# A four-layer graph kernel: order of the first loads, W1·a as one block, later weight sums, six last graphs turned on TensorE, and bv added to x3 early

## Chip, core and metric

The kernel runs on one core of one Trainium2 chip. The metric is the time of one execution on the device in microseconds, the median of several runs. "Before" took 2840.91 us (three runs, 2839.7 to 2845.04). Everything is float32.

## What is computed

128 graphs of 128 nodes with 512 features pass through four layers. Each layer adds its result to its input and normalizes over the features:

```python
# layer 0: out[n] = max over nodes of relu(adj @ x), with a shift b
x = layernorm(x + L0(x, adj, b))
# layer 1: graph attention; h = x @ W, s1 = h @ a1, s2 = h @ a2
e   = leaky_relu(s1[:, None] + s2[None, :], 0.2) * adj
x = layernorm(x + elu(softmax(e) @ h + beta * h))
# layer 2: graph convolution
x = layernorm(x + (adj @ x) @ weight + bias)
# layer 3: attention with 8 heads of 64, masked where adj == 0
q, k, v = x @ Wq + bq, x @ Wk + bk, x @ Wv + bv
x = layernorm(x + softmax(q @ k.T / 8 + mask) @ v)
```

## The kernel before

One graph fills the 128 partitions (nodes), with 512 features along the row. There is no loop over layers in the code. A small planner (`Plan`, L23 to L124) holds a list of TensorE steps (`l0`, `zT`, `z`, `yT`, `y`, `xT`, q/k/v, `sc`, `pT`, `avT`, `av`; L935 to L957), a place for each in the order, an assumed cost, and the marks and buffers that it needs. Each step is a generator. It issues its matmuls and then asks for engine time with `yield dve(...)`, `act(...)`, `pool(...)` or `sp(issue, landing)`. The planner advances an imagined clock and so fixes, while the program is built, in which order each engine's instructions stand. On the chip every engine runs its own list in order and waits for data alone; the planner's microseconds are no waits there. A buffer given back with `plan.give` is free in the plan, and the real dependency is kept by semaphores.

**Start.** The five weight matrices (1 MB each) are loaded by ScalarE's queue right away, in one DMA each (`load_w`, L214). The rows `a_bc`, `bias2_bc` and `bv_bc` (each broadcast to 128 partitions, 256 KB) and the small columns are loaded by POOL's queue. SP loads adj and the graphs, two x buffers deep (`load_x`, L208). `w1_a` (L274 to L301) computes W1·a1 and W1·a2, so that layer 1's s1 and s2 come straight from x: for each half and each of four blocks of W1, a multiply with a row sum on VectorE (L285), a diagonal matrix of that column (L288) and a product with ones (L289), and at the end a copy to `wa_bc` (L295). `weight_sums` (L307) prepares q, k and v for a seven-product form of the 2x2 block product: four POOL adds for each matrix (L324), Wq scaled first on ScalarE (L316).

**Layers 0 to 2.** `l0` (L373) multiplies with adj, takes the maximum (L381), adds it (L387), normalizes, and forms s2 and s1 (L400). `attention` (L435) makes the softmax (L439 to L455). `l1_zT` and `l1_out` give z = (att x) W1 (L482, L496, L506 to L512). `l2_yT` and `l2_out` do layer 2 (L536, L496, L578). `layernorm` (L330) is a VectorE statistic (L333, L335), three small POOL steps (L338, L340, L342) and one ScalarE pass (L344). Its result x3 is stored to HBM in the layout of the turn and kept there for the residual.

**Layer 3.** Four graphs form a group. `seven` computes q, k and v of a group in seven steps each (L660), from x transposed (`xTh`) and POOL differences of it (`T`, L566). `l3_scores` (L758) writes the scores of a graph to a score bank in PSUM, of which there is one (`"sc": 1`), adds the mask on VectorE into `pr` (L780), takes the row maxima (L786) and runs eight exp on ScalarE (L790). For all but the last `LATE` = 4 graphs the weights are transposed by a *turn* (`turn`, L346): a DMA to HBM (L354), a DMA back (L358), and a 32x32 block transpose on VectorE (L365). There is one `pr` buffer of this kind. `l3_avT` (L835) then forms the output transposed (L843), copies it (L855) and turns it back the same way. `fetch` (L610) brings x3 back from HBM as `x3r` (L614). POOL scales by the softmax sums (L868), adds x3r (L869) and adds bv (L871); then come the last normalization and the store (L877).

For the last four graphs `pr` lies in a buffer of `xTh`, TensorE transposes it (`l3_pT`, L822), ScalarE and VectorE copy it out of PSUM (L829, L831), and `l3_av` (L880) computes the output untransposed (L890) with the sums as a 65th column, divides (L902, L903), and adds x3r and bv on POOL (L913, L916).

Of the kernel before, what the change touches and what calls it, by code (L numbers as in the profile page):

```python
# [9 lines left out]
F32 = mybir.dt.float32  # L10
# [4 lines left out]
P = 128  # L15
# [112 lines left out]
def kernel(  # L128
# [25 lines left out]
    NQ = P // Q  # L154
    EARLY, LATE = GB, GB

# [16 lines left out]
    small = ctx.enter_context(tc.tile_pool(name="small", bufs=5))  # L173
    plan = Plan({**sb_bufs, **ps_bufs, **hbm_bufs, "va": NV})

# [24 lines left out]
    def sp(us, landing):  # L200
        return ("SP", us, landing)
# [6 lines left out]
    def load_x(b):  # L208
        x0[b] = yield from get("x0", [P, C], f"x0_{b}")
        yield sp(0.35, 2.5 if b > 2 else 7.0)  # L210
        nc.sync.dma_start(out=x0[b], in_=x[b])
        plan.mark(("x0", b))

    def load_w(w, name):  # L214
        t = const.tile([P, NCC, C], F32, tag=name, name=name)
        nc.scalar.dma_start(out=t, in_=w.rearrange("(c p) f -> p c f", p=P))
        return t

    def load_row(v, name):
        t = const.tile([P, C], F32, tag=name, name=name)  # L220
        nc.gpsimd.dma_start(out=t, in_=v.partition_broadcast(P))
        return t

# [5 lines left out]
    a_flat = a1.rearrange("f o -> (f o)")  # L229
    a_bc = []  # L230
    for i in range(2):
        t = sb_tile("xp", [P, C], f"a_bc{i}")
        nc.gpsimd.dma_start(out=t, in_=a_flat[i * C : (i + 1) * C].partition_broadcast(P))
        a_bc.append(t)
        plan.left["xp"] -= 1
    b0_col = load_col(b0, 1, "b0_col")
    w1_sb = load_w(w1, "w1_sb")
# [4 lines left out]
    w2_sb = load_w(w2, "w2_sb")  # L242
    wq_sb = load_w(wq, "wq_sb")
    wk_sb = load_w(wk, "wk_sb")
    wv_sb = load_w(wv, "wv_sb")
    bias2_bc = load_row(bias2, "bias2_bc")
    bv_bc = load_row(bv, "bv_bc")
    bq_col = load_col(bq, NCC, "bq_col")
    bk_col = load_col(bk, NCC, "bk_col")


# [19 lines left out]
    wa_bc = [const.tile([P, C], F32, tag=f"wa_bc{i}", name=f"wa_bc{i}") for i in range(2)]  # L271
    plan.engine["DVE"] = 7.0

    def w1_a():  # L274

        yield sp(0.0, 9.0)
        for i in (1, 0):
            yield "mm"
            ps = ps_tile("mm", f"ps_wa{i}")
            for c in range(NCC):  # L280
                junk = yield from get("junk", [P, C], f"wa_junk{i}_{c}")
                dg = yield from get("att", [P, P], f"wa_diag{i}_{c}")
                yield dve(1.1)
                col = small.tile([P, 1], F32, tag="col", name=f"wa_col{i}_{c}")
                nc.vector.scalar_tensor_tensor(  # L285
                    junk, w1_sb[:, c, :], 1.0, a_bc[i], ALU.mult, ALU.mult, accum_out=col
                )
                nc.vector.tensor_scalar(dg, ident, col, None, ALU.mult)  # L288
                nc.tensor.matmul(ps[:, c * P : (c + 1) * P], ones, dg, start=True, stop=True)  # L289
                plan.give("junk")  # L290
                plan.give("att")
            plan.give("xp")
            yield ("PE", 0.5, 0.0)
            yield dve(0.7)
            nc.vector.tensor_copy(wa_bc[i], ps)  # L295
# [275 lines left out]
    def l2_out(b):  # L571
        s = st[b]
        yT = s.pop("yT")
        ps = product(f"y_{b}", lambda c: yT[:, c * P : (c + 1) * P], lambda c: w2_sb[:, c, :])
        plan.give("yT")
        xp = yield from get("xp", [P, C], f"xp2_{b}")
        yield dve(0.7)
# [32 lines left out]
    def fetch(b, tag):  # L610
# [147 lines left out]
    def l3_scores(b):  # L758
# [54 lines left out]
    def l3_pT(i):  # L813
# [9 lines left out]
        plan.give("xTh")  # L823
        s["pT"] = sb_tile("pT", [P, H, P], f"pT_{b}")
# [10 lines left out]
    def l3_avT(b):  # L835
# [44 lines left out]
    def l3_av(i):  # L880
# [12 lines left out]
        if hh == 0:  # L893
            s["o"] = sb_tile("oT", [P, H, HD], f"o_{b}")
        else:
# [19 lines left out]
        plan.give("oT")  # L915
        nc.gpsimd.tensor_tensor(xp, xp, bv_bc, ALU.add)  # L916
        yield from last(b, xp)
# [12 lines left out]
    def av_waits(b):  # L930
# [23 lines left out]
            lambda i: av_waits(late_av(i)),  # L954
            lambda i: {"mm": 1, "oT": 1 - i % 2}, l3_av,
        ),
# [3 lines left out]
    for b in range(sb_bufs["x0"]):  # L960
        plan.at(1.0, load_x(b))
    plan.at(0.0, w1_a())
    for n, w in (("q", wq_sb), ("k", wk_sb), ("v", wv_sb)):
        plan.at(0.0, weight_sums(n, w))
# [32 lines left out]
```

## Time and profile before

| what | value |
|---|---|
| median of three runs | 2840.91 us |
| profiled execution | 2842.72 us, its span 2840.7 us |
| granted TensorE clock, mean | 0.985 |
| TensorE busy | 2736.5 us, 96% of the span |
| VectorE busy | 2268.5 us, 80% |
| ScalarE busy | 1577.9 us, 56% |
| POOL busy | 1397.2 us, 49% |
| DMA | 395.42 MB, mean 139 GB/s |

The span runs from the first to the last instruction of the core. In the profile's names PE is TensorE, DVE is VectorE, ACT is ScalarE, POOL is GpSimd and SP the engine that issues most DMAs; a "q" behind a name is an engine's queue. A row of the timeline gives the start, the length, the engine, the line, the operation with output and input, and in brackets the idle time ahead of it and what ended that.

### The profile page before, as it was taken

The page shows a single profiled execution, that of the slowest core. Times are in us where ns is not written, and L with a number is a line of the kernel's source. Part 1 is how long each engine was busy: PE and PEld are TensorE (multiplying, and loading weights), DVE is VectorE, ACT ScalarE, POOL GpSimd, SP SyncE. Part 2 cuts the span into 40 slices and gives each one's busy share as a digit, 9 for nine tenths or more (in the row PEclk, how much of TensorE's full clock was granted, in tenths as well). Part 3 has the DMA queues.
Part 4 walks back from the last instruction along what each step waited for, and adds up shares of the span by engine and source line. Part 5 has one row for each costly group of instructions (what it writes and reads, how often), then busy time and mean ns, then how long its engine had stood idle before and what let it go on. Part 6 is the DMA issues. An engine that isn't in the chain of part 4 may idle for free.

```text
span 2840.7 us, 43148 instructions
## 1 busy us (share of the span) xinstructions
PE 2736.5 (96%) x13901; PEld 1939.3 (68%) x13901; DVE 2268.5 (80%) x4290; ACT 1577.9 (56%) x4205; POOL 1397.2 (49%) x2198
## 2 busy tenths in 40 slices
PE   4999999999999999999999999999999999999985
PEld 2667767667667677777666767767677767777674
DVE  6678787788888888788888878778888788778755
ACT  2555555555555655555555556555555555555543
POOL 4435455455455555445554545545445555445534
PEclk8999999999999999999999999999999999999996
DMA  3224444454444454454454544544454544444443
GB/s 114 59 71 132 141 152 141 129 159 142 140 149 149 135 166 140 136 155 134 147 150 143 160 146 132 163 143 137 136 162 139 166 133 147 150 136 143 135 133 122
DMA packets 462178, 395.42 MB, mean 139 GB/s; under 512 B 88832, under 2 KB 378752, under 8 KB 461952
## 3 DMA queue, kind: packets, MB, share of 16 engines
q1 hardware_dynamic: 458864, 386.37, 44.6%
q10 hardware_dynamic: 2640, 5.24, 0.5%
q8 instruction: 110, 1.80, 0.3%
q0 software_dynamic: 448, 1.05, 0.1%
q14 instruction: 116, 0.95, 0.1%
HBM read 219.75 MB, written 172.82 MB: 138 GB/s over the span
## 4 chain that ended last, share of the span: by engine, by line
PE 83%; DVE 11%; DMA 2%; POOL 1%; issue 1%; ACT 1%; SPq 0%; POOLq 0%; DVEq 0%; ACTq 0%
PE ps_z L496 14%; PE ps_y L496 13%; PE ps_k_chain L660 7%; PE ps_q_chain L660 7%; PE ps_v_chain L660 7%; PE ps_av L843 4%; PE ps_zT L482 4%; PE ps_sc L764 4%; PE ps_k_pair L660 4%; PE ps_yT L536 4%; PE ps_v_pair L660 3%; PE ps_q_pair L660 3%; PE psA L378 3%; DVE pT L365 2%; PE ps_q_first L660 2%; PE ps_v_first L660 2%
## 5 line engine op out<-in xcount | busy, mean ns | idle before, releaser
L338 POOL TENSOR_SCALAR ve<-mv 128x1 f32<-128x1 f32 x512 | 129.9, 254 | 819.8 <-DVE mv L335 739.4
L790 ACT ACTIVATE pr<-pr,nm 128x128 f32<-128x128 f32 x1024 | 397.8, 392 | 126.1 <-DVE nm L786 124.6
L496 PE MATMUL ps_y<-w_sb,yT 128*128 128x512 f32 x1024 | 463.6, 595 | 3.9 <-ACT yT L542 3.3
L496 PE MATMUL ps_z<-w_sb,zT 128*128 128x512 f32 x1024 | 463.3, 595 | 1.0 <-ACT zT L488 1.0
L344 ACT ACTIVATE x<-xp,nmr,rstd 128x512 f32<-128x512 f32 x384 | 310.5, 809 | 159.9 <-POOL nmr L342 158.6
L333 DVE BATCH_NORM_STATS2 stats<-xp 128x6 f32<-128x512 f32 x512 | 345.1, 674 | 37.7 <-ACT xp L387 22.6
L496 PEld LDWEIGHTS ps_z<-w_sb,zT 128*128 128x128 f32 x1024 | 193.2, 191 | 203.2 <-issue 196.6
L496 PEld LDWEIGHTS ps_y<-w_sb,yT 128*128 128x128 f32 x1024 | 190.4, 190 | 204.8 <-issue 195.6
L340 POOL TENSOR_TENSOR rstd<-ve,nhalf 128x1 f32<-128x1 f32 x512 | 302.2, 590 | 42.6
L868 POOL TENSOR_TENSOR xp<-xp,rd 128x512 f32<-128x512 f32 x124 | 131.5, 1061 | 368.5 <-DVE xp L365 207.1
L365 DVE STREAM_TRANSPOSE pT<-turn_pr 128x1024 f32<-128x1024 f32 x124 | 254.1, 2049 | 2.3 <-DMA turn_pr<-turn_hbm_pr 2.3
L400 DVE SCALAR_TENSOR_TENSOR junk<-x,wa_bc 128x512 f32<-128x512 f32 x256 | 196.0, 766 | 53.2 <-ACT x L344 51.7
L506 ACT ACTIVATE elu_r<-ps_z 128x512 f32<-128x512 f32 x128 | 76.1, 594 | 248.2 <-PE ps_z L496 247.9
L522 POOL TENSOR_TENSOR x2b<-x,bias_bc 128x512 f32<-128x512 f32 x128 | 165.4, 1292 | 83.9 <-ACT x L344 83.8
L790 ACT ACTIVATION_READ_ACCUMULATOR pr<-pr,nm 128x1 f32 x992 | 187.7, 189 | 0.0
L764 PEld LDWEIGHTS ps_sc<-kTh,qTh 64*128 64x128 f32 x2048 | 128.3, 192 | 66.6 <-issue 37.4
L342 POOL TENSOR_SCALAR nmr<-mv,rstd 128x1 f32<-128x1 f32 x512 | 146.6, 286 | 53.0
L764 PE MATMUL ps_sc<-kTh,qTh 64*128 64x128 f32 x2048 | 153.2, 290 | 17.0 <-DVE pr L780 16.9
L510 DVE SCALAR_TENSOR_TENSOR xp<-ps_z,x 128x512 f32<-128x512 f32 x128 | 88.1, 688 | 100.3 <-ACT elu_r L506 100.2
L871 POOL TENSOR_TENSOR xp<-xp,bv_bc 128x512 f32<-128x512 f32 x124 | 163.0, 1314 | 9.7
L780 DVE TENSOR_TENSOR pr<-ps_sc,mask 128x1024 f32<-128x1024 f32 x128 | 154.8, 1209 | 15.0 <-DMA turn_hbm_pr<-pr 7.3
L869 POOL TENSOR_TENSOR xp<-xp,x3r 128x512 f32<-128x512 f32 x124 | 161.6, 1304 | 9.7
(147 smaller groups left out, 5863.8 us busy)
## 6 DMA issues: line engine op xcount, KB each, us to landing
turn_hbm_pr<-pr SPq DMA_DIRECT2D x124, 512.0 KB
turn_pr<-turn_hbm_pr SPq DMA_DIRECT2D x124, 512.0 KB
x<-in_x_dram SPq DMA_DIRECT2D x128, 256.0 KB
out_dram<-xp SPq DMA_DIRECT2D x128, 256.0 KB
turn_hbm_x<-x SPq DMA_DIRECT2D x124, 256.0 KB
turn_x<-turn_hbm_x SPq DMA_DIRECT2D x124, 256.0 KB
turn_hbm_o<-oT SPq DMA_DIRECT2D x124, 256.0 KB
turn_o<-turn_hbm_o SPq DMA_DIRECT2D x124, 256.0 KB
```

What stands on the lines that cost most here:

```text
L333: nc.vector.bn_stats(stats, src)
L340: nc.gpsimd.tensor_tensor(rstd, ve, nhalf, ALU.pow)
L344: nc.scalar.activation(dst, src, AF.Identity, bias=nmr, scale=rstd)
L365: nc.vector.transpose(dst.rearrange("p n (c a) -> p a n c", a=NQ), t)
L400: nc.vector.scalar_tensor_tensor(junk, x1, 1.0, wa_bc[i], ALU.mult, ALU.mult, accum_out=col)
L496: nc.tensor.matmul(ps, lhsT(c), rhs(c), start=(c == 0), stop=(c == NCC - 1))
L522: nc.gpsimd.tensor_tensor(xb, x2, bias2_bc, ALU.add)
L660: nc.tensor.matmul(ps[:, m, :], lhsT, rhs, start=fresh and m + k == 0, stop=m + k == 2, skip_group_check=not fresh)
L764: nc.tensor.matmul(ps[:, h % 2, f, :], heads["q", g][j // 2][r : r + HD, f, j % 2 * P : (j % 2 + 1) * P], heads["k", g][j // 2][r : r + HD ...
L790: nc.scalar.activation(pr_h[:, i], pr_h[:, i], AF.Exp, bias=nm[:, i : i + 1], accum_out=None if late else den[:, i : i + 1])
L869: nc.gpsimd.tensor_tensor(by_block(b, xp), by_block(b, xp), s.pop("x3r"), ALU.add)
L871: nc.gpsimd.tensor_tensor(xp, xp, bv_bc, ALU.add)
```

## The change

It has six parts.

1. `a_bc` (a2's half first) moves to SP's queue, ahead of the graphs. W1 stays first on ScalarE's queue, in four DMAs, one for each block of rows. W2, Wq, Wk, bias2, Wv and bv are issued on ScalarE's queue by a planned generator `later_loads`.
2. `w1_a` does, for each half, four multiplies with row sums, one multiply of a broadcast identity with the four columns, one product with ones of 512 columns, and the copy.
3. The weight sums are planned at 44, 52 and 60 us (before: all at 30) and with gaps between the adds.
4. `LATE` is 6: graphs 122 and 123 are transposed by TensorE too. The first four late graphs keep `pr` in the room of W1 and W2 once the last z and the last y are issued (tag `"w"`).
5. bv is added to `x3r` on POOL in `fetch`, as soon as it is there; L871 and L916 go.
6. The output `o` of a late graph takes a buffer of `x2` (two) where it took `oT` (one).

```diff
-    EARLY, LATE = GB, GB
+    EARLY, LATE = GB, 6
...
-    plan = Plan({**sb_bufs, **ps_bufs, **hbm_bufs, "va": NV})
+    plan = Plan({**sb_bufs, **ps_bufs, **hbm_bufs, "va": NV, "w": 0})
...
-        yield sp(0.35, 2.5 if b > 2 else 7.0)
+        yield sp(0.35, 2.5 if b > 1 else 5.5 + b)
...
-    for i in range(2):
-        t = sb_tile("xp", [P, C], f"a_bc{i}")
-        nc.gpsimd.dma_start(out=t, in_=a_flat[i * C : (i + 1) * C].partition_broadcast(P))
+    for i in (1, 0):
+        a_bc[i] = sb_tile("xp", [P, C], f"a_bc{i}")
+        nc.sync.dma_start(out=a_bc[i], in_=a_flat[i * C : (i + 1) * C].partition_broadcast(P))
         plan.left["xp"] -= 1
+    w1_sb, w1_in = load_w(w1, "w1_sb")
+    for c in range(NCC):
+        nc.scalar.dma_start(out=w1_sb[:, c], in_=w1_in[:, c])
...
+    def later_loads():
+
+        for us, dst, src in (
+            (9.5, w2_sb, w2_in), (1.0, wq_sb, wq_in), (4.0, wk_sb, wk_in), (1.0, bias2_bc, bias2_in), (4.0, wv_sb, wv_in),
+            (1.0, bv_bc, bv_in),
+        ):
+            yield sp(0.0, us)
+            yield act(0.06)
+            nc.scalar.dma_start(out=dst, in_=src)
...
-        yield sp(0.0, 9.0)
+        yield sp(0.0, 6.5)
         for i in (1, 0):
+            junk = yield from get("junk", [P, C], f"wa_junk{i}")
+            dg = yield from get("oT", [P, NCC, P], f"wa_diag{i}")
+            yield dve(3.9)
+            cols = small.tile([P, NCC], F32, tag="cols", name=f"wa_cols{i}")
+            for c in range(NCC):
+                nc.vector.scalar_tensor_tensor(
+                    junk, w1_sb[:, c, :], 1.0, a_bc[i], ALU.mult, ALU.mult, accum_out=cols[:, c : c + 1]
+                )
+            nc.vector.tensor_tensor(
+                dg,
+                ident.unsqueeze(1).to_broadcast([P, NCC, P]),
+                cols.unsqueeze(2).to_broadcast([P, NCC, P]),
+                ALU.mult,
+            )
...
+            nc.tensor.matmul(ps, ones, dg.rearrange("p c n -> p (c n)"), start=True, stop=True)
...
-        yield sp(0.0, 30.0)
+        yield sp(0.0, {"q": 44.0, "k": 52.0, "v": 60.0}[n])
...
             nc.gpsimd.tensor_tensor(dst, x_, y_, op)
+            yield sp(0.0, 0.7)
...
+        if b == B - 1:
+            plan.give("w")
+            plan.give("w")
...
-        st[b]["x3r"] = xb if b < EARLY else xb.rearrange("p (b n c) -> p b n c", b=NQ, c=Q)
+        s = st[b]
+        s["x3r"] = xb if b < EARLY else xb.rearrange("p (b n c) -> p b n c", b=NQ, c=Q)
+        yield pool(1.32)
+        nc.gpsimd.tensor_tensor(s["x3r"], s["x3r"], by_block(b, bv_bc), ALU.add)
...
-        pr = yield from get("xTh" if late else "pr", [P, H * P], f"pr_{b}")
+        i = b - (B - LATE)
+        if 0 <= i < 4:
+
+            yield "w"
+            pr = (w1_sb, w2_sb)[i // 2][:, i % 2 * 2 : i % 2 * 2 + 2, :].rearrange("p c n -> p (c n)")
+        else:
+
+            pr = yield from get("xTh" if late else "pr", [P, H * P], f"pr_{b}")
...
-        yield pool(4.0)
+        yield pool(2.4)
...
-        nc.gpsimd.tensor_tensor(xp, xp, bv_bc, ALU.add)
...
-            s["o"] = sb_tile("oT", [P, H, HD], f"o_{b}")
+            s["o"] = sb_tile("x2", [P, H, HD], f"o_{b}")
...
-        yield pool(2.6)
+        yield pool(1.3)
```

The block that gives `"w"` stands in `l1_out` and again in `l2_out`.

More of the change, by code (lines that the diff above doesn't have):

```diff
@@ L214, in load_w @@
     def load_w(w, name):
-        t = const.tile([P, NCC, C], F32, tag=name, name=name)
-        nc.scalar.dma_start(out=t, in_=w.rearrange("(c p) f -> p c f", p=P))
-        return t
+        return const.tile([P, NCC, C], F32, tag=name, name=name), w.rearrange("(c p) f -> p c f", p=P)
     def load_row(v, name):
         t = const.tile([P, C], F32, tag=name, name=name)
-        nc.gpsimd.dma_start(out=t, in_=v.partition_broadcast(P))
-        return t
+        return t, v.partition_broadcast(P)
     def load_col(v, n, name):
@@ L229 @@
     a_flat = a1.rearrange("f o -> (f o)")
-    a_bc = []
-    for i in range(2):
-        t = sb_tile("xp", [P, C], f"a_bc{i}")
-        nc.gpsimd.dma_start(out=t, in_=a_flat[i * C : (i + 1) * C].partition_broadcast(P))
-        a_bc.append(t)
+    a_bc = [None, None]
+    for i in (1, 0):
+        a_bc[i] = sb_tile("xp", [P, C], f"a_bc{i}")
+        nc.sync.dma_start(out=a_bc[i], in_=a_flat[i * C : (i + 1) * C].partition_broadcast(P))
         plan.left["xp"] -= 1
+    w1_sb, w1_in = load_w(w1, "w1_sb")
+    for c in range(NCC):
+        nc.scalar.dma_start(out=w1_sb[:, c], in_=w1_in[:, c])
     b0_col = load_col(b0, 1, "b0_col")
-    w1_sb = load_w(w1, "w1_sb")
     ident = const.tile([P, P], F32, tag="ident", name="ident")
@@ L241 @@
     nc.gpsimd.dma_start(out=beta_col, in_=beta.partition_broadcast(P))
[L242 to L247, printed above, removed]
     bq_col = load_col(bq, NCC, "bq_col")
     bk_col = load_col(bk, NCC, "bk_col")
+    (w2_sb, w2_in), (wq_sb, wq_in), (wk_sb, wk_in), (wv_sb, wv_in) = (
+        load_w(w, f"{n}_sb") for n, w in (("w2", w2), ("wq", wq), ("wk", wk), ("wv", wv))
+    )
+    (bias2_bc, bias2_in), (bv_bc, bv_in) = load_row(bias2, "bias2_bc"), load_row(bv, "bv_bc")
+    def later_loads():
[6 more added lines that the diff above has]
+            nc.scalar.dma_start(out=dst, in_=src)
     ones = const.tile([P, P], F32, tag="ones", name="ones")
@@ L271 @@
     wa_bc = [const.tile([P, C], F32, tag=f"wa_bc{i}", name=f"wa_bc{i}") for i in range(2)]
-    plan.engine["DVE"] = 7.0
+    plan.engine["DVE"] = 6.0
     def w1_a():
-        yield sp(0.0, 9.0)
+        yield sp(0.0, 6.5)
         for i in (1, 0):
+            junk = yield from get("junk", [P, C], f"wa_junk{i}")
[11 more added lines that the diff above has]
+                ALU.mult,
+            )
+            plan.give("junk")
+            plan.give("xp")
             yield "mm"
             ps = ps_tile("mm", f"ps_wa{i}")
[L280 to L293, printed above, removed]
+            yield ("PE", 1.0, 0.0)
+            nc.tensor.matmul(ps, ones, dg.rearrange("p c n -> p (c n)"), start=True, stop=True)
+            plan.give("oT")
             yield dve(0.7)
@@ L575, in l2_out @@
         plan.give("yT")
+        if b == B - 1:
+            plan.give("w")
+            plan.give("w")
         xp = yield from get("xp", [P, C], f"xp2_{b}")
@@ L822, in l3_pT @@
                 nc.tensor.transpose(pss[e][:, f * P : (f + 1) * P], pr[:, c : c + P], ident)
-        plan.give("xTh")
+        if i >= 4:
+            plan.give("xTh")
         s["pT"] = sb_tile("pT", [P, H, P], f"pT_{b}")
@@ L914, in l3_av @@
         plan.give("x1")
-        plan.give("oT")
-        nc.gpsimd.tensor_tensor(xp, xp, bv_bc, ALU.add)
+        plan.give("x2")
         yield from last(b, xp)
@@ L954 @@
             lambda i: av_waits(late_av(i)),
-            lambda i: {"mm": 1, "oT": 1 - i % 2}, l3_av,
+            lambda i: {"mm": 1, "x2": 1 - i % 2}, l3_av,
         ),
@@ L962 @@
     plan.at(0.0, w1_a())
+    plan.at(0.0, later_loads())
     for n, w in (("q", wq_sb), ("k", wk_sb), ("v", wv_sb)):
```

## The prediction, made before the changed kernel was built or run

> **What bounds the kernel now.** I read the page first, then busy time by stage, then the two ends instruction by instruction. Stage table of TensorE (stage, length, busy time, instructions, granted clock, DMA share, GB/s):
> ```profile
> 0.00:100.00 100.00, 64.22 (x206) 0.86 0.31 102
> 100.00:400.00 300.00, 298.58 (x1441) 1.00 0.38 113
> ...
> 2720.00:2776.00 56.00, 48.21 (x274) 0.94 0.39 123
> 2776.00:2841.00 65.00, 29.93 (x225) 0.64 0.37 118
> ```
> From 100 to 2720 us TensorE is busy for 2594 of 2620 us (the nine stages added) at clock 0.99 to 1.00: there the kernel is bound by matmuls, and the change removes none. The idle time lies at the ends: 36 us of the first 100, 43 us of the last 121, and part of the busy time there is at half clock. An edit pays if it lets the matmul stream start sooner or the end follow it sooner.
>
> Start, from the timeline (start, length, engine, line, what, idle before):
> ```profile
> 10.14 0.69 DVE L285 SCALAR_TENSOR_TENSOR wa_junk<-w_sb,a_bc 128x512 f32<-128x512 f32 x1 [4.52 <-DMA a_bc<-in_L_gnn_a_dram]
> ...
> 30.78 0.68 DVE L400 SCALAR_TENSOR_TENSOR junk<-x,wa_bc 128x512 f32<-128x512 f32 x1
> ...
> 33.34 1.78 DVE L400 SCALAR_TENSOR_TENSOR junk<-x,wa_bc 128x512 f32<-128x512 f32 x1
> ...
> 35.05 0.68 DVE L295 COPY wa_bc<-ps_wa 128x512 f32<-128x512 f32 x1
> ...
> 42.20 1.24 DVE L442 TENSOR_TENSOR e<-e,adj_sb 128x128 f32<-128x128 f32 x1
> ...
> 50.70 0.29 DVE L442 TENSOR_TENSOR e<-e,adj_sb 128x128 f32<-128x128 f32 x1
> ...
> 53.10 5.37 PE L496 MATMUL ps_z<-w_sb,zT 128*128 128x512 f32 x8 [0.25 <-ACT zT L488]
> ```
> The first z product starts at 53.10 us and the stream is nearly unbroken afterwards. Before it, VectorE is the bound: it waits for `a_bc` until 10.14, does eight separate W1·a steps that end only at 35.05, and between 31.6 and 48.3, while POOL runs its twelve weight sums (L324), the same instruction takes 1.78 instead of 0.68 and 1.24 instead of 0.29.
>
> End:
> ```profile
> 2776.05 1.16 PE L764 MATMUL ps_sc<-kTh,qTh 64*128 64x128 f32 x16
> ...
> 2786.99 1.23 DVE L780 TENSOR_TENSOR pr<-ps_sc,mask 128x1024 f32<-128x1024 f32 x1 [4.21 <-DMA turn_hbm_pr<-pr]
> ...
> 2811.61 2.00 DVE L365 STREAM_TRANSPOSE pT<-turn_pr 128x1024 f32<-128x1024 f32 x1
> ...
> 2825.12 1.08 DVE L365 STREAM_TRANSPOSE xp<-turn_o 128x512 f32<-128x512 f32 x1 [2.72 <-DMA turn_o<-turn_hbm_o]
> ...
> 2836.62 0.81 ACT L344 ACTIVATE xp<-xp,nmr,rstd 128x512 f32<-128x512 f32 x1 [0.51 <-POOL nmr L342]
> ```
> The last projection ends at 2776. The scores of graph 123 (2776.05) sit in the one score bank until 2786.99, because its mask add needs the one `pr` buffer, which is held until graph 122's turn has left for HBM. Graphs 124 to 127 queue behind. Graph 123 then makes two round trips through HBM, and work of 126 and 127 stands behind its transposes on VectorE and its adds on POOL. 61 us pass between the last projection and the last normalization.
>
> **Part by part: loads.** The bytes wanted first (adj 64 KB, two `a_bc` of 256, W1 1024, two x of 256) are 2.1 MB. The DMA row shows about 350 to 400 GB/s once running, from about 2 us: 5.6 us, plus about 2 us until the semaphore. x0 lands near 9 to 10 (before: 8.93; it now stands behind the two `a_bc` on SP's queue, whose issue costs SP some 0.4 each, the L205 row, and whose 512 KB go first; graphs 2 and 3 follow behind them, but their loads wait for x0's buffers anyway, until L387), `a_bc` near 6 to 7 (before: 10.14). W2 and Wq are not really held back: the planner's 9.5 and 1.0 us are no waits on the chip, only places in ScalarE's order, and by its sums (9.65, 11.0) they stand ahead of ScalarE's first instruction (due 11.6). So both are issued right behind W1. Only Wk, bias2, Wv and bv come later. That still helps ScalarE, whose issue of Wv was blocked for 7.86 us, to 11.41, ahead of L387. The Trainium skill, "DMA: Bandwidth & Descriptors", Rules for kernel authors, speaks against W1 in four pieces: one DMA of 1 MiB or more, and its fit gives each DMA about 2.0 us fixed, by which four 256 KB pieces in turn would take 4 × 2.6 = 10.4 us instead of 4.4. The trace's row has 256 KB loads from several queues in flight together at 350 GB/s and more; I take no cost, at most 2 us.
>
> **W1·a as a block.** Before, 8 × (0.69 + 0.29) plus gaps in which VectorE stood behind psA or the ones product. After, per half: 4 × 0.7, one broadcast multiply, a product, the 0.68 copy. The multiply is not in the trace: between 0.69 (L578, the same size) and 4 × 0.29 = 1.16; I take 0.7 as size sets it. The ones product is one pair of 128x512 like psA, 2.05 at half clock. First half about 7 to 11 us, second done near 22, then scores, exp, the att transpose, zT (2.08) and a copy, as now (some 10 us from L400 to z): first z at about 32 instead of 53, 21 us sooner.
>
> **Weight sums later.** They leave 31 to 48 and go to 44 to 69 by the planner, one every 2.15 us. What they cost VectorE now, row against row: three L400 3.1, L300 1.1, two L441 1.4, two L442 1.9, two L408 1.4, one L288 0.4: 9.3 us. The Trainium skill, "SBUF — State Buffer", Who interferes with whom, speaks against calling this a gain: GpSimd and a VectorE instruction with two SBUF inputs take one port pair, one blocking the other for a whole instruction, so moving the twelve only moves the block; by it up to 12 × 1.3 to 1.7 = 17 us would fall in the new place. By the rows it is at most 9.3, and VectorE is busy about 70% from 60 to 100 (27.8 of 40), so its slack takes most. I charge 3 us (0 to 9). First use of the sums: before 89.9 us (q_chain); some 20 sooner is 70, when q and k are due (53, 61); v is late by nothing, its first step was at 102.
> Starting sooner also finds less work heaped up: before, at 53 us, four graphs had their layer 0 done. VectorE's work to that state (four graphs to 3.5 us, three attentions, W1·a) is some 30 us, so it is reached near 41, not 32. I charge 2 us for gaps between. Start: 21 − 3 − 2 = **16 us** (9 to 21).
>
> **Graphs 122 and 123 by TensorE.** Removed: two `pr` turns and two `oT` turns (eight DMAs), two 2.0 and two 1.1 transposes on VectorE. Added: 16 transposes on TensorE (8 took 1.04 warm, L630; 1.9 cold, L822), copies of 0.59 and 0.68, and av of 128x65 in place of avT (3.94 for two graphs at half clock, against 1.98 for one): nothing net on TensorE. W1's and W2's room is free from 2701 and 2720, where the last z and y read it, so no new wait. Scores of 121 still stand behind `pr` (L780 at 2755.2), so 122 can't start sooner than its 2758.8. After that nothing waits for HBM: 123 follows at about 2763 instead of 2776, and 124 to 127 at VectorE's pace. VectorE is then the bound. From 2756: masks and maxima 6 × 2.44, copies 6 × 0.68, outputs 6 × 1.16, statistics 6 × 0.87, q/k/v sums 3.5, graphs 119 to 121 some 10.3, L786 1.2: 46 us, about the 45.9 busy now, of which the 85 us to the end use 54%. Without a gap the last statistics end at 2802; POOL 1.1, ScalarE 0.8 and the store 3.3 (2837.4 to 2840.7) give 2808. Before, gaps doubled it. I allow 10%, 5 us: end at 2813, **28 us** sooner (18 to 36).
>
> **bv into x3r.** Per graph one POOL add of 1.27 (L869, same size) moves ahead; the sum stays. At the end it takes 1.3 off the last chain (in the 2808 already: the chain there is one add). The new add makes POOL wait in order for the x3r transfer; behind it stand the small normalization steps (L338 to L342) that ScalarE, then TensorE, wait for. x3r's landing isn't listed; 256 KB of the same kind took 4.47 (turn_x), the planner allows 5.35, and POOL is 49% busy and already stands at L868 for 207 us. I take 0, bounds −4 and +10. Order in the middle changes with the plan; its idle time is 26 us, ±4.
>
> **Sum.** Profiled execution 2842.72 (span 2840.7 plus 2.0): minus 16 minus 28 is 2798.7. The median shown lies 1.8 below it: **2797**.
>
> **Rivals.**
> 1. The start is given back (0.15): the weight sums meet a VectorE that has just become the bound. The start then gives 7; total 35: 2806. For it: the block rule above. Against: VectorE's 30% of slack from 60 to 100, where TensorE is full already.
> 2. The end is still turned through HBM (0.18): graph 121 keeps two round trips (from its scores at 2739 to its output at 2803 now), and its transposes stand in VectorE's queue before late work. Tail gain 14; total 30: 2811.
> 3. Both ends come out full (0.10): VectorE gapless, sums hidden: 22 + 38 = 60: 2781.
> 4. Slower (0.04): POOL waits for x3r in the middle of every one of 122 graphs and TensorE runs dry behind it. It decides from 44 / 122 = 0.36 us of TensorE idle per graph; at 0.6 it costs 73, ending at 2870. Against: in the middle TensorE waits for VectorE's transposes only (19 us in 17 waits) and never for POOL.
> 5. No change (0.03): the stall of rival 4 near 0.36 us. That the loads are not held back is counted above.
>
> **Numbers.** Likeliest, as summed, 0.50: 2797. Range from rival 3's side to rival 2's with their bounds: 2779 to 2817. Faster by over 0.2% (5.7 us, about what a measurement here can tell) 0.93, within 0.03, slower 0.04.
>
> **What would show it.** First z at 30 to 36 us; L400 at 0.68 before 44 us; L285 from about 7; POOL's L324 after 44, with slow VectorE rows there. At the end, no L780 waiting for turn_hbm_pr after graph 121's; VectorE busy 80% or more from the last projection on; last normalization about 30 us after it. Wrong if TensorE idles over 40 us between 100 and 2720, if POOL's new add shows long waits for x3r, or if the first z stays after 42.

## The result and the profile after

Median of four runs: 2803.32 us after (2802.51 to 2804.39), 2842.81 before beside it (four runs, the three behind 2840.91 among them); ratio 0.9862 (95% interval 0.9845 to 0.9879), 39.5 us less. The forecast was 2797, in a range of 2779 to 2817. The profiled execution took 2803.4 us, its span 2801.6. The diff moves the lines: L285 is now L289, L295 L306, L324 L335, L365 L377, L400 L412, L496 L508, L333 L345, L344 L356, L455 L467, L512 L527, L630 L651, L780 L807, L843 L871, and L913 L940; the early bv add is L639.

The stages, TensorE alone (stage, length, busy time, instructions, granted clock, DMA share, GB/s), in the kernel after:

```profile
0.00:100.00 100.00, 71.09 (x240) 0.91 0.33 106
100.00:400.00 300.00, 297.69 (x1456) 1.00 0.39 115
400.00:2680.00 2280.00, 2262.19 (x11585) 1.00 0.48 145
2680.00:2736.00 56.00, 50.75 (x276) 0.94 0.39 124
2736.00:2802.00 66.00, 48.90 (x355) 0.85 0.41 129
```

TensorE's idle time fell from 36 to 29 us in the first 100 us, and the last 122 us hold 22 idle us instead of 43. Between 100 and 2680 us it is 20.1 us, where it was 25.8 before. So a third place has changed, the middle, in which the prediction let nothing happen. Comparing when each graph's scores start, and when the last v product ends (2776.13 before, 2758.94 after), splits the span's gain of 39.1 us:

| stretch | gain, us | predicted |
|---|---|---|
| up to graph 0's scores (178.5 before, 167.7 after) | 10.8 | 16 |
| from there to the last v product | 6.4 | 0 |
| last v product to the end (64.6 before, 42.7 after) | 21.9 | 28 |

The start, timeline of the kernel after:

```profile
6.38 0.69 DVE L289 SCALAR_TENSOR_TENSOR wa_junk<-w_sb,a_bc 128x512 f32<-128x512 f32 x1 [0.76 <-DMA a_bc<-in_L_gnn_a_dram]
10.80 3.36 PE L390 MATMUL psA<-x,adjT 128*128 128x512 f32 x4 [6.53 <-DMA x<-in_x_dram]
10.94 0.69 DVE L289 SCALAR_TENSOR_TENSOR wa_junk<-w_sb,a_bc 128x512 f32<-128x512 f32 x1 [1.42 <-DMA w_sb<-in_L_gnn_W_dram]
...
15.05 0.69 DVE L306 COPY wa_bc<-ps_wa 128x512 f32<-128x512 f32 x1
...
20.97 2.08 PE L390 MATMUL psA<-x,adjT 128*128 128x512 f32 x2 [1.63 <-DMA x<-in_x_dram]
22.84 1.53 PE L303 MATMUL ps_wa<-wa_diag,ones 128*128 128x512 f32 x2
...
24.55 0.68 DVE L306 COPY wa_bc<-ps_wa 128x512 f32<-128x512 f32 x1
...
36.62 1.55 PE L508 MATMUL ps_z<-w_sb,zT 128*128 128x512 f32 x2 [0.46 <-ACT zT L500]
```

`a_bc` is there at 6.38, but W1's last block only at 10.94. The product with ones is short, yet each time it stands in TensorE's list behind the adj products of two graphs: the first half ends at 15.7, and the second waits for graph 3's x (20.97) to end at 25.2. The first z starts at 36.62, 16.5 us sooner than before.

The end, timeline of the kernel after:

```profile
2722.99 1.23 DVE L807 TENSOR_TENSOR pr<-ps_sc,mask 128x1024 f32<-128x1024 f32 x1 [4.45 <-DMA turn_hbm_pr<-pr]
...
2742.41 1.21 DVE L807 TENSOR_TENSOR pr<-ps_sc,mask 128x1024 f32<-128x1024 f32 x1
...
2745.14 1.16 PE L785 MATMUL ps_sc<-kTh,qTh 64*128 64x128 f32 x16
...
2788.68 0.42 DVE L930 TENSOR_TENSOR o<-ps_av,rd 128x256 f32<-128x256 f32 x1
...
2791.12 1.26 POOL L639 TENSOR_TENSOR x3r<-x3r,bv_bc 128x512 f32<-128x512 f32 x1
...
2792.35 2.48 POOL L940 TENSOR_TENSOR xp<-o,x3r 128x512 f32<-128x512 f32 x2
2793.64 0.69 DVE L345 BATCH_NORM_STATS2 stats<-xp 128x6 f32<-128x512 f32 x1 [4.53 <-POOL xp L940]
...
2797.51 0.81 ACT L356 ACTIVATE xp<-xp,nmr,rstd 128x512 f32<-128x512 f32 x1 [0.51 <-POOL nmr L354]
```

The first two rows are the mask adds of graphs 120 and 121, 19 us apart, and graph 122's scores (third row) come right after the second. Behind them no mask add waits for HBM. VectorE is busy for 26.16 of the 30 us from 2759 to 2789 and writes the last output at 2789.1. Then it waits 4.53 us, because POOL still has a bv add (L639) and small normalization steps ahead of the two last output adds.

### The profile page after: what moved, and what is told of

It reads as the page before. It is cut to its first block, busy times and chain, and to the rows that moved or that the text cites. A ratio compares the mean times of both kernels' runs of the same rounds, so it can differ in the third digit from the quotient of the medians.

```text
span 2801.6 us, 42968 instructions
## 1 busy us (share of the span) xinstructions
PE 2730.6 (97%) x13905; PEld 1936.2 (69%) x13905; DVE 2276.3 (81%) x4288; ACT 1573.6 (56%) x4189; POOL 1388.1 (50%) x2192
## 4 chain that ended last, share of the span: by engine, by line
PE 85%; DVE 11%; POOL 1%; DMA 1%; issue 1%; ACT 1%; SPq 0%; DVEq 0%; POOLq 0%; ACTq 0%
PE ps_z L508 14%; PE ps_y L508 13%; PE ps_q_chain L681 7%; PE ps_k_chain L681 7%; PE ps_v_chain L681 7%; PE ps_av L871 4%; PE ps_sc L785 4%; PE ps_zT L494 4%; PE ps_k_pair L681 4%; PE ps_v_pair L681 4%; PE ps_q_pair L681 3%; PE psA L390 3%; PE ps_yT L551 3%; PE ps_q_first L681 2%; DVE pT L377 2%; PE ps_v_first L681 2%
## 5 line engine op out<-in xcount | busy, mean ns | idle before, releaser
L508 PE MATMUL ps_y<-w_sb,yT 128*128 128x512 f32 x1024 | 463.8, 596 | 0.5 <-ACT yT L557 0.5
L508 PE MATMUL ps_z<-w_sb,zT 128*128 128x512 f32 x1024 | 462.6, 594 | 1.6 <-ACT zT L500 1.1
L817 ACT ACTIVATE pr<-pr,nm 128x128 f32<-128x128 f32 x992 | 387.1, 393 | 77.8 <-DVE nm L813 76.8
L356 ACT ACTIVATE x<-xp,nmr,rstd 128x512 f32<-128x512 f32 x384 | 311.0, 810 | 187.8 <-POOL nmr L354 184.4
L345 DVE BATCH_NORM_STATS2 stats<-xp 128x6 f32<-128x512 f32 x512 | 345.0, 674 | 23.2 <-ACT xp L399 14.7
L508 PEld LDWEIGHTS ps_z<-w_sb,zT 128*128 128x128 f32 x1024 | 192.4, 190 | 211.0 <-issue 203.2
L508 PEld LDWEIGHTS ps_y<-w_sb,yT 128*128 128x128 f32 x1024 | 190.7, 190 | 201.6 <-issue 193.2
L352 POOL TENSOR_TENSOR rstd<-ve,nhalf 128x1 f32<-128x1 f32 x512 | 298.6, 583 | 42.7
L377 DVE STREAM_TRANSPOSE pT<-turn_pr 128x1024 f32<-128x1024 f32 x122 | 249.7, 2047 | 0.0
L412 DVE SCALAR_TENSOR_TENSOR junk<-x,wa_bc 128x512 f32<-128x512 f32 x256 | 208.5, 814 | 50.7 <-ACT x L356 49.0
L639 POOL TENSOR_TENSOR x3r<-x3r,bv_bc 128x512 f32<-128x512 f32 x128 | 170.5, 1332 | 90.3 <-DMA x3r<-turn_hbm_x 89.2
L871 PE MATMUL ps_av<-pT,va 128*64 128x128 f32 x1952 | 135.4, 281 | 21.6 <-DVE pT L377 17.1
L871 PEld LDWEIGHTS ps_av<-pT,va 128*64 128x64 f32 x1952 | 105.9, 138 | 72.9 <-issue 30.6
```

The source lines that it names most:

```text
L345: nc.vector.bn_stats(stats, src)
L352: nc.gpsimd.tensor_tensor(rstd, ve, nhalf, ALU.pow)
L356: nc.scalar.activation(dst, src, AF.Identity, bias=nmr, scale=rstd)
L377: nc.vector.transpose(dst.rearrange("p n (c a) -> p a n c", a=NQ), t)
L412: nc.vector.scalar_tensor_tensor(junk, x1, 1.0, wa_bc[i], ALU.mult, ALU.mult, accum_out=col)
L508: nc.tensor.matmul(ps, lhsT(c), rhs(c), start=(c == 0), stop=(c == NCC - 1))
```

## The experiments

Twelve kernels, each timed beside the kernel before, whose median lay between 2841.3 and 2843.0 us. First the change in three pieces.

### Parts 1 to 3 alone (loads, W1·a, weight sums)

```diff
-    EARLY, LATE = GB, 6
+    EARLY, LATE = GB, GB
...
-        nc.gpsimd.tensor_tensor(s["x3r"], s["x3r"], by_block(b, bv_bc), ALU.add)
...
+        nc.gpsimd.tensor_tensor(xp, xp, bv_bc, ALU.add)
```

(The diff is against the kernel after.)

> The kernel before with the first three parts alone (loads, W1 a as a block, weight sums later); the end and bv as before. Theory 1 (the start gives what the shift of the stream after 170 us shows, some 11 us, the end 22, the rest of some 6 comes from order in the middle): 2832, with the first z near 37 us. Theory 2 (the start gives the 16 of the prediction and the missing 5 were lost to bv's add waiting on POOL): 2827. Rival (the whole 16.5 by which the first z is sooner is kept when the middle is unchanged): 2826.

Measured 2830.12 us, ratio 0.9958 (0.9943 to 0.9972): 12.6 us gained. First z at 37.45; graph 0's scores 9.0 us sooner, the last v product 12.3 sooner, and 64.6 us from there to the end, as before. These parts are worth 12, not 16: 9 of them are there at graph 0, 3 come in the middle, and they are kept to the end.

### Parts 4 and 6 alone (graphs 122 and 123)

```diff
-    EARLY, LATE = GB, GB
+    EARLY, LATE = GB, 6
...
+            yield "w"
+            pr = (w1_sb, w2_sb)[i // 2][:, i % 2 * 2 : i % 2 * 2 + 2, :].rearrange("p c n -> p (c n)")
...
-            s["o"] = sb_tile("oT", [P, H, HD], f"o_{b}")
+            s["o"] = sb_tile("x2", [P, H, HD], f"o_{b}")
```

> The kernel before with the six last graphs on TensorE, their weights in W1's and W2's room and o in x2's buffers; start and bv as before. Theory 1: the end gives 22 by itself, 2821, from the last v product to the end of the span 43 us instead of 65. Rival (the end only works because bv's add is off its last chain too): 1.3 to 2.5 less, 2823. The prediction's 28 would be 2815.

Measured 2820.15 us, ratio 0.9921 (0.9907 to 0.9936): 22.5 us gained. From the last v product to the end there are 37.7 us instead of 64.6, 27 less and close to the 28 of the sum. But that product now comes at 2779.65, 3.5 us later: the late graphs' scores and transposes have moved ahead of the last projections, and TensorE is busy for 2648.3 us from 100 us to that product instead of 2642.5. The prediction counted how much shorter the end gets, not what its work displaces in front of it.

### Part 5 alone (bv into x3r)

```diff
+        nc.gpsimd.tensor_tensor(s["x3r"], s["x3r"], by_block(b, bv_bc), ALU.add)
...
-        nc.gpsimd.tensor_tensor(xp, xp, bv_bc, ALU.add)
```

> The kernel before with bv added to x3r early and nothing else. Theory 1 (the 6 us that the middle of the changed kernel gained belong to this part, since a graph's last POOL steps are shorter by one add): 2837, TensorE's idle time from 100 to 2720 us down from 26 to 20. Rival A (order luck of the plan): anything within 4 of 2843. Rival B (POOL's wait for x3r, 89 us over 49 times in the changed kernel, reaches TensorE): 2846 or more, with TensorE waiting for normalizations in the middle.

Measured 2822.41 us, ratio 0.9932 (0.9916 to 0.9949): 20.3 us gained by the part that was put at nothing. The first z is where it was (52.98), the end is as long as it was (64.5), but the last v product comes 22 us sooner. TensorE's waits between 170 and 2680 us (total, times, longest), the kernel before:

```profile
PE ps_av L843 <- DVE pT L365: 19.0, 17, 2.6
```

and with part 5 alone:

```profile
PE ps_av L846 <- DVE pT L365: 9.7, 12, 1.8
```

The same product stands at L843 there and at L846 here. TensorE between 100 and 2680 us, the kernel before and then part 5 alone (stage, length, busy time, instructions, granted clock, DMA share, GB/s):

```profile
100.00:2680.00 2580.00, 2554.16 (x12993) 1.00 0.47 141
100.00:2680.00 2580.00, 2567.07 (x13075) 1.00 0.46 142
```

So its idle time there fell from 25.8 to 12.9, and another 5 us of idle time went between 2680 us and the last v product. The middle was not simply bound by matmuls; a good part of those waits could be taken away. The parts alone add up to 12.6 + 22.5 + 20.3 = 55 us, the whole change gives 39.5.

### Why bv is worth anything: order, or less work?

Part 5 takes a POOL add out of the stretch before the last statistics, and it also changes the planner's costs, and with them every engine's order. Two kernels separate these. The first is the kernel before with both bv adds left out, in the same order; it leaves bv out of the output.

```diff
-        nc.gpsimd.tensor_tensor(xp, xp, bv_bc, ALU.add)
```

> The kernel before with bv's add left out altogether (the output lacks bv) and every planned cost as it was: each engine's list is the one of before, less 128 POOL adds. It splits what the early add alone gave, 20 us. Theory 1 (the gain is the shorter last POOL stretch of each graph: the store waits less on SP's queue, so the turns behind it go sooner): 2823, TensorE's wait for pT in the middle down from 19 to about 10 us. Theory 2 (the gain is the other order that the planner finds, since the stretch's cost goes from 4.0 to 1.32 and 2.4): 2841, with 1.3 from the last chain alone.

Measured 2825.66 us, ratio 0.9941 (0.9926 to 0.9956): 17.3 us gained without any change of order. The waits for `pT` fell to 12.7 us in 14 times, where theory 1 had about 10. The second has part 5's order, and a multiply by ones of the same size put back in the old place:

```diff
+        nc.gpsimd.tensor_tensor(
+            xp.rearrange("p (n c) -> p n c", c=P), xp.rearrange("p (n c) -> p n c", c=P),
+            ones.unsqueeze(1).to_broadcast([P, NCC, P]), ALU.mult,
+        )
```

> The kernel with bv added early and nothing else, and with a POOL multiply by ones of the same size put back where bv's add was: order of the early add on every engine, the old length of POOL's last stretch. Theory 1 (shorter stretch): 2840. Theory 2 (order): 2823 to 2825.

Measured 2846.28 us, ratio 1.0014 (1.0007 to 1.0021): the gain is gone, so the new order doesn't bring it by itself. What the order is worth can't be read off exactly, because this kernel has one POOL instruction in each graph more than the kernel before (2326 in all, against 2198). What is paid for, in either order, is a 128x512 POOL instruction of 1.3 us at that place in each graph: 17.3 us in the old order, 23.9 in the new one.

How does it cost? One way is POOL's own list: all behind it comes later. Another is seen in VectorE's rows (total, mean ns, idle). Before:

```profile
L441 DVE SCALAR_TENSOR_TENSOR e<-e 128x128 f32<-128x128 f32 x128 | 80.2, 627 | 4.4
L442 DVE TENSOR_TENSOR e<-e,adj_sb 128x128 f32<-128x128 f32 x128 | 64.8, 506 | 4.4
```

without the adds, in the same order:

```profile
L441 DVE SCALAR_TENSOR_TENSOR e<-e 128x128 f32<-128x128 f32 x128 | 66.5, 520 | 4.4
L442 DVE TENSOR_TENSOR e<-e,adj_sb 128x128 f32<-128x128 f32 x128 | 50.0, 390 | 4.4
```

The same instructions are over 100 ns shorter. VectorE's busy time falls from 2268.5 to 2235.2 us, 0.26 us for each of the 128 adds left out. Part 5 itself moves the add and doesn't remove it, and there VectorE's busy time is only 4.4 us less than before (2264.1): the slow rows move too, from L441 and L442 (483 and 438 ns then) mostly to L439, L455 and L400 (384 to 454, 402 to 448 and 766 to 799). The last kernel tells the two ways apart, with five tiny POOL steps in place of the multiply:

```diff
+        for _ in range(5):
+            nc.gpsimd.tensor_scalar(xp[:, 0:1], xp[:, 0:1], 1.0, None, ALU.mult)
```

> The version with part 5 alone (2822.4 us) and, in the old place of bv's add, five tiny POOL steps on one column (128x1, times 1.0, some 0.25 us each by the rows of the normalization's small steps) instead of the 128x512 multiply by ones that took the time to 2846.3. POOL's queue is lengthened by about the same 1.3 us per graph, but hardly any data is read. Theory 1 (a longer stretch ahead of the last statistics is what costs, whatever POOL does in it): about 2846 us as with the multiply. Theory 2 (the large POOL instruction costs because VectorE's instructions with two inputs run slower beside it: in the version with the multiply VectorE was busy 29.6 us longer than without, the adj multiply 492 instead of 438 ns, the leaky step 589 instead of 483): VectorE's busy time stays within 8 us of 2264 and the time is about 2822 to 2828 us.

Measured 2835.81 us, ratio 0.9978 (0.9968 to 0.9987), between the two. VectorE is not slowed (busy 2262.9 us; part 5 alone has 2264.1, the version with the multiply 2293.7). The version with the multiply, then the one with the tiny steps:

```profile
L441 DVE SCALAR_TENSOR_TENSOR e<-e 128x128 f32<-128x128 f32 x128 | 75.4, 589 | 4.4
L442 DVE TENSOR_TENSOR e<-e,adj_sb 128x128 f32<-128x128 f32 x128 | 63.0, 492 | 4.4
...
L441 DVE SCALAR_TENSOR_TENSOR e<-e 128x128 f32<-128x128 f32 x128 | 59.0, 461 | 4.4
L442 DVE TENSOR_TENSOR e<-e,adj_sb 128x128 f32<-128x128 f32 x128 | 56.9, 444 | 4.4
```

The profiled executions of these kernels, split at the last v product:

| kernel | last v product ends | from there to the end |
|---|---|---|
| before | 2776.1 | 64.6 |
| no bv adds, old order | 2764.9 | 59.3 |
| part 5 alone | 2754.0 | 64.5 |
| part 5 and tiny steps | 2763.0 | 70.7 |
| part 5 and multiply | 2774.0 | 70.7 |

Neither theory holds alone. Of the 23.9 us that the multiply costs over part 5 alone, 13.4 are also paid with steps that hold POOL's list about as long but read almost nothing; the other 10.5 go with VectorE's slower rows. By the table, the end loses 6 us with either, and up to the last v product the tiny steps cost 9 us and the multiply 20. The split is rough: the tiny steps occupy POOL a little longer (142 us busy and 52 between them, against 163 and 10), and reckoned against the kernel before that ran beside each, it is 14.8 and 8.8.

How POOL's longer list reaches TensorE is not settled. VectorE waits longer for POOL's last instruction ahead of the statistics (the two "POOL xp" numbers, in us), with part 5 alone and with the tiny steps:

```profile
L333 DVE BATCH_NORM_STATS2 stats<-xp 128x6 f32<-128x512 f32 x512 | 344.5, 673 | 32.0 <-ACT xp L387 19.9 <-POOL xp L872 7.7 <-POOL xp L915 3.0
L333 DVE BATCH_NORM_STATS2 stats<-xp 128x6 f32<-128x512 f32 x512 | 345.4, 675 | 80.3 <-POOL xp L875 42.6 <-ACT xp L387 25.9 <-POOL xp L921 9.9
```

But SP, whose list holds the transfers of the turns behind the store, also waits longer for the last normalization before it can issue that store: 175.7 us in all with part 5 alone, 194.7 with the tiny steps and 199.4 with the multiply. No run parts these two.

### The change without part 5

Alone, bv is worth 20; what is it worth beside the rest?

```diff
-        nc.gpsimd.tensor_tensor(s["x3r"], s["x3r"], by_block(b, bv_bc), ALU.add)
...
+        nc.gpsimd.tensor_tensor(xp, xp, bv_bc, ALU.add)
```

> The kernel after with part 5 undone: bv is again added at the end of every graph by a POOL instruction of its own (the x3r add goes), everything else as after. Alone on the kernel before, part 5 was worth 20.3 us; parts 1 to 3 alone 12.7 and parts 4 and 6 alone 22.5. Theory 1 (the worth of part 5 does not depend on the other parts): 2803.3 + 20.3 = 2823.6 us. Theory 2 (the middle of the kernel is set by the planned order, which every part shifts, and the tail part has already taken the place of the shorter end): only what parts 1 to 4 and 6 give alone is lost from before, 2842.8 - 35.2 = 2807.6 us, so part 5 is worth about 4 here; between graph 0 and the last v product the shift against the kernel before then stays within 3 us of its start value of 9 to 11.

Measured 2807.97 us, ratio 0.9878 (0.9862 to 0.9895), as theory 2 had it: part 5 is worth 4.7 us here, and the other two pieces add up (35 us). The starts of the scores show where the rest went. At graph 104 the whole change is 21.0 us ahead of the kernel before, this version 12.6; at graph 121 it is 10.1 and 13.0. What part 5 wins in the middle is lost again before graph 121; why was not tried. Split as in the table above, this version gains 9.0 us up to graph 0, loses 1.5 from there to the last v product and gains 27.5 behind it, against 10.8, 6.4 and 21.9 with part 5. So the end gives almost the forecast 28 where the work in front of it is later, and less where it is sooner.

### The weight sums

The kernel after with the twelve POOL adds left out; the seven-product form then reads blocks of the weights in place of the sums, at the same cost on every other engine.

```diff
-            nc.gpsimd.tensor_tensor(dst, x_, y_, op)
```

> The changed kernel without the twelve POOL adds of the weight sums: they are left out and blocks of the raw weights are used in their place, so q, k and v are not the reference's; the plan's order is the same. Theory 1 (the start lost 5 us after the first z because the adds stand in POOL's queue between the normalization steps, 55 to 88 us, and TensorE waited for x3): the shift of the stream against before grows from 11 to 15 or 16 at 170 us, total 2798, no TensorE waits for x3 at 65 to 88. Rival (VectorE itself is the bound there, POOL's adds cost it only the port): VectorE rows shorten by some 5 us in total but TensorE's waits stay, total 2802. Rival 2 (the loss comes from the order of the first graphs, not from POOL): 2803.

Measured 2799.53 us, ratio 0.9846 (0.9831 to 0.986): 3.8 us below the kernel after, though the intervals overlap. TensorE's idle time from 36.6 to 170 us falls from 7.4 to 3.8 us, though its first z comes 1.3 us later (37.87). In the kernel after the sums ran from 54.9 to 87.9, in between the small normalization steps in POOL's list:

```profile
57.27 1.22 DVE L527 SCALAR_TENSOR_TENSOR xp<-elu_r,xp 128x512 f32<-128x512 f32 x1
...
68.95 0.66 PE L651 MATMUL ps_xT<-ident,x 128*128 128x128 f32 x4 [1.88 <-ACT x L356]
...
71.17 1.17 DVE L467 SCALAR_TENSOR_TENSOR att<-pe,rd,beta_id 128x128 f32<-128x128 f32 x1
```

VectorE's rows are slower there (1.22 for 0.69, 1.17 for 0.35), but in all its busy time is only 2.3 us more than without the sums (2276.3 against 2274.0). TensorE waits for ScalarE's pass of a normalization that POOL has served late; without the sums these waits at L651 (3.6 us in two) are gone.

The same sums some 25 us later in the plan; the first two steps of q, k and v, which read none of them, go without:

```diff
-            keys = [("sums", n)]
+            keys = [("scaled" if i < 2 else "sums", n)]
```

> The changed kernel; the first two steps of q, k and v, which read raw weight blocks, no longer wait for the sums, and the sums are planned at 70, 76 and 86 us. Theory 1 (POOL's queue at 55 to 88 us cost the start some 4 us, as leaving the sums out gave back): most of it comes back, 2800, without a TensorE wait for x3 at 65 to 90. Rival (the adds do the same harm wherever they stand while the first group's chain is being filled): 2803, waits for T or x3 at 95 to 130.

Measured 2823.62 us, ratio 0.9936 (0.9921 to 0.9951): 20 us slower than the kernel after, against both theories. Graph 24's scores are 11 us ahead of the kernel before, graph 112's are 16 us behind it, and TensorE's waits for `pT` between 170 and 2680 us have grown to 22.9 us in 24 times. A changed plan at 50 us gives another order in all that follows, and that order cost more than the edit was about. Which pairs of instructions make it worse was not tried.

### W2 and Wq really held back

```diff
-            (9.5, w2_sb, w2_in), (1.0, wq_sb, wq_in),
+            (13.0, w2_sb, w2_in), (1.0, wq_sb, wq_in),
```

> The kernel after with one number changed: W2's planned place is 13.0 instead of 9.5 us, so that ScalarE issues W2 and Wq (2 MB) only behind its first instruction for graph 0, and not at 3.7 and 6.3 us. Theory 1 (the two loads take bandwidth from adj, W1 and the x of graphs 0 to 3): 2 MB at about 350 GB/s are 6 us of DMA time; the last W1 block and x0, which landed at 10.9 and 10.8, land 2 to 3 us sooner, the x waits of graphs 2 and 3 shrink likewise, first z at about 33.5 instead of 36.6, time about 2800.5 us. Rival (the way to the first z is VectorE's and POOL's work and ScalarE's table load, not the bytes): first z within 1 us of 36.6 and the time within 1.5 us of 2803.3; W2 arriving later costs nothing as its first product is far behind.

Measured 2805.63 us, ratio 0.9868 (0.9853 to 0.9883). x0 and W1's last block land 0.2 to 0.5 us sooner, the first z comes at 37.33, and the time is 2.3 us above the kernel after, a little more than the rival allowed. Nothing is gained: W2 and Wq, now issued at 15.1 and 15.5 us, are out of the way of x0 and W1, but graph 3's x comes at 21.70 instead of 20.97.

### The end: earlier x3r, and the gate of `pr`

x3r of the late graphs fetched when their scores are issued, the last two into `x2b`:

```diff
+        if late:
+            plan.at(plan.end, fetch(b, late_x3r(b)))
```

> The changed kernel; x3r of the six last graphs is fetched when their scores are issued, not after their exps, with the last two in x2b's buffers, so that bv's add for graphs 126 and 127 (at 2787.2 and 2791.1 now, just ahead of the adds of o) leaves the end of POOL's list. Theory 1 (these two adds stand on the last chain): 2.5 us less, 2801, and POOL ahead of the last two adds idle. Rival (VectorE ends the chain, at 2789.1, and POOL would wait for it): 2803.

Measured 2801.98 us, ratio 0.9862 (0.9845 to 0.9878): last v product to the end 40.9 us instead of 42.7, the time 1.3 lower, within the spread. The bv adds now stand ahead, and from VectorE's last output to the end of the last statistics it takes 2.3 us instead of 6.7. But VectorE's last output itself comes later, 32.7 us after the last v product instead of 30.2.

The same with eight late graphs, so that graphs 120 and 121 don't use `pr` either:

```diff
-    EARLY, LATE = GB, 6
+    EARLY, LATE = GB, 8
...
-        if 0 <= i < 4:
+        if 0 <= i < 4 or i == 7:
...
+        if i == 0:
+            plan.give("w")
```

> Kernel after with x3r fetched early for the late graphs (that version alone: 2802.0 us), and eight instead of six late graphs turned by TensorE: graphs 120 to 123 get their probabilities in W1's and W2's room, 124 to 126 in the three xTh buffers, 127 in W1's first half again. Theory 1 (the one pr buffer, whose three mask adds of 119 to 121 follow each other 17 to 20 us apart because each waits for the turn through HBM of the one before, still holds up graph 122 in the kernel after): the mask adds of 120 and 121 wait for nothing, the scores of 122 start at about 2737 instead of 2745, the last v product to the span's end shrinks from 40.9 to about 35, time about 2796 us. Rival (VectorE is without a gap from the last v product on, so opening the gate only moves work ahead of the last projections on TensorE): the stretch after the last v product shrinks but the last v product comes later by as much; 2800 to 2804 us.

Measured 2801.94 us, ratio 0.9855 (0.9841 to 0.987). The gate is open:

```profile
2711.59 1.16 PE L788 MATMUL ps_sc<-kTh,qTh 64*128 64x128 f32 x16
2712.80 1.23 DVE L813 TENSOR_TENSOR w_sb<-ps_sc,mask 128x1024 f32<-128x1024 f32 x1 [0.34 <-PE ps_sc L788]
2714.60 1.16 PE L788 MATMUL ps_sc<-kTh,qTh 64*128 64x128 f32 x16
```

Graph 120's mask add waits for nothing, 121's scores follow 3 us later (2714.60 instead of 2728.8), 122's at 2719.6 instead of 2745.1. The stretch after the last v product is 35.0 us, as theory 1 said, but that product ends at 2764.19, 5.2 us later, with 7.6 us more of matmuls between 100 us and it. The time is that of the rival: work that can't wait any more goes in front of the last projections. No kernel of these beats the kernel after by more than the spread.

## Why the prediction came out right, and where its steps did not

- **Loads.** `a_bc` at 6.38 (6 to 7) and W2 and Wq issued right behind W1 (3.71 and 6.29 us) came as worked out, and holding them back gains nothing. x0 was 0.8 us later than the upper end. For W1's four pieces a cost of "at most 2 us" stood open; what no term of the sum had is that the last piece lands only at 10.94, 10.2 us after the first was issued. The 10.4 us named against the pieces are an estimate from the fit of "DMA: Bandwidth & Descriptors", which that page states for DMAs issued by GpSimd (Anatomy of one DMA — SWDGE (gpsimd) path), while W1 goes by ScalarE's queue. Measured and estimate agree here, but x, `a_bc`, W2 and Wq were in flight too, so the run doesn't show the pieces going in turn. In the kernel before, W1 in one DMA was there at 10.14 at the latest; one DMA with the new order was not tried.
- **W1·a.** The multiply took 0.69, as by its size, and the ones product 1.02 and 1.53 instead of 2.05. (That the 2.05 was due to half clock the profile doesn't show: where psA took it in the kernel before, at 8.96 us, the granted clock reads 1.00.) The step that failed is "First half about 7 to 11 us, second done near 22": it added up VectorE's own times and left out W1's last block, and the place of the ones product behind the adj products in TensorE's list. Measured 15.7 and 25.2, so the first z came at 36.6 and not 32, just outside the 30 to 36 given as a sign: 4.6 of the 21 us.
- **Gaps and sums.** Charged were 2 and 3. TensorE idles 7.4 us between the first z and 170 us, 5.5 more than before; without the sums it is 3.8. At graph 0's scores the start gives 10.8 (16.5 less 5.7), of which taking the sums away returns 2.8. The 3 held. The rule of "SBUF — State Buffer", Who interferes with whom, with up to 17 us for the twelve sums, was far too high here: VectorE's busy time shows 2.3. (Its product was off, too: 12 × 1.3 to 1.7 us is 15.6 to 20.4.) Rival 1 fell by its cause, though by its number the 10.8 lies nearer to its 7 than to 16. The slow VectorE rows were expected, POOL's late normalization steps were not.
- **The end.** No mask add waits for HBM after 121's, VectorE is full (87%) for 30 us after the last v product, as forecast, though from there to the end it is at 66%, and the last normalization comes 38.6 us after that product, not about 30. "Without a gap the last statistics end" 26 us after the last projection, with the allowance 31, is the step that failed: VectorE's last output is written after 30.2 us, but the last statistics end only after 36.8, at 2795.8. Between them lies the way through POOL's list, where a bv add and six small steps stand ahead, and back to VectorE, which the sum put beside VectorE's work and not behind it. These 6 us are the difference between 28 and 21.9. They show where the time passes, not what freeing POOL returns: with the bv adds taken out of the way only 1.8 came back, and without part 5 the end gave 27.5. Rival 2 fell: graph 121's transposes are not last.
- **bv.** "I take 0, bounds −4 and +10" is the step that was wrong. It weighed only the wait that the new add brings. That wait is there (89.2 us on POOL, in 49 times), which the prediction had named as a sign of being wrong; but no wait of TensorE between 170 and 2680 us ends with POOL, so rival 4 fell. Overlooked was what the add had cost in its old place in each graph: 1.3 us of POOL's list ahead of the last statistics, with slow VectorE rows beside it. Out of that place it is worth 20 us alone, and 4.7 beside the other parts.
- **The middle.** "its idle time is 26 us, ±4" took a sum of waits for a fixed thing. It was 12.9 with part 5 alone, 20.1 after, and 43.5 with the sums planned later. The 6.4 us that the middle gave come with part 5, for without it the middle lost 1.5.
- **The sum.** 2797 was 6.3 us low. Start and end were overrated by 5.2 and 6.1 us, the middle underrated by 6.4: that makes 4.9, and that the middle's gain stood in for part of the missing 11.3 is luck. The rest comes from the 1.8 us taken off for the median; with one more run the kernel before has its median at the profiled time (2842.8), and so has the kernel after. The mechanism of both ends was the forecast one: W1·a was done at 25.2 instead of 35.7 us and the first z came 16.5 us sooner, and at the end the mask adds behind graph 121's no longer wait for HBM.

## What to carry to other kernels

When VectorE is 80% busy beside a full TensorE, don't take a big GpSimd instruction to be free just because GpSimd is idle half the time. Leave one out in the same order and see. Price an in-order step at the place that it has in each engine's list, with what stands before it, and end a tail's sum with the last result's own way through every engine. When a planner sets the order, the parts' gains don't add up: measure each alone and all but one, and compare when the same graph starts.

## What was not expected of the chip

A 128x512 POOL add with two inputs (1.3 us) lengthened VectorE's work by 0.26 us on average (33.3 us for 128 of them, in the same order), most of it in 128x128 steps whose inputs lie in SBUF (506 to 390 ns); five 128x1 POOL steps in the same place lengthened it by nothing (2262.9 against 2264.1 us). The Trainium skill, "SBUF — State Buffer", Who interferes with whom, names such a shared port; that one-column steps leave VectorE's rows as they are, and what the conflict costs per instruction, are this case's numbers.
